# Reading token tiles spread by quarters and norming them in place, with a new order for the first attention step

## The chip, the cores and the metric

The kernel runs on one core of one Trainium2 chip. The metric is the device time of one execution in microseconds (us); smaller is better. Engines are named as in the profile: PE is TensorE (matmuls; PEld is its weight load), DVE is VectorE, ACT is ScalarE, POOL is GpSimd, SP is SyncE, which only issues DMAs. A "q" behind an engine's name is its sequencer, which issues DMAs and waits.

## The reference

Everything is float32; B = 2 sequences of S = 1024 tokens with H = 512 features, so 2048 tokens.

```
xn  = (x - mean(x)) / sqrt(var(x) + 1e-5)              # layernorm over the features
q, k, v = split(xn @ w_qkv.T + b_qkv)
s   = softmax(q @ k.T / sqrt(512)) @ v @ w_out.T + b_out
logits = xn @ router_w + router_b                      # 8 experts, the best two, softmax of the two
e_i = silu(xn @ expert_w[i] + expert_b[i])
c   = w_1 * e_1 + w_2 * e_2                            # weighted sum of the two chosen experts
y   = xn + c @ proj_w + proj_b
out = x + s * silu(norm_w * y / sqrt(mean(y*y) + 1e-6))
```

## The kernel before, in words

Tokens are worked in 16 tiles of 128. Each engine runs its instructions in the order in which the code writes them (`keep_order` ties each to the one before), so the order of the work is written out by hand, and what stands early in an engine's queue and waits holds all that stands behind it. DMAs are issued from SP, ACT and POOL in the same written order.

**Prologue (0 to 91 us).** SP loads the value and output weights (`wv_in`, `wo`), the query and key weights in spread form (`wZ`) and the token tiles `x`. TensorE transposes the value weights (`turn_wv`, L382) and multiplies them with the output weights (`product_vo`, L391: eight products, `hc` 0 to 3 for `n` 0 and then 1), so that values come out already projected; ACT copies each product from PSUM to `rwvo` (L402). `rwvo` also holds the router's weights and one more column. PSUM tiles of the pool `ps_mm` go round over four banks in written order.

The layernorm of a pair of tiles is `stats`, `shifts`, `rows` (L314 to L359). VectorE takes `bn_stats` and `bn_aggr` of each tile, ACT the root, VectorE reciprocal and shift; `rows` has ACT write the normed tile to `xn` with the features in another order (`in_turn`), and SP store it twice: to `xn_d`, from which the experts gather their tokens, and to the scratch `xn_s`, from which it comes back as `xz` with the tokens spread. For the first four tiles (`DIRECT`) there is no scratch: ACT writes a second normed copy `xw`, and TensorE transposes it. `turn_x` (L368) makes `xnT`, the tile with features on partitions: from `xz` by a 32x32 block transpose on VectorE (`turn`, L118), for the first four tiles from PSUM by a copy. `x` has 8 buffers, `xn` has 5 and `xz` has 6, so loads and norms wait for buffers.

`value_side` (L443) multiplies a tile by `rwvo` in two halves of 256 and 265 columns, PSUM tile `pv` with two buffers; `keep_values` (L458) copies the values to `vo` on ACT and adds the router's bias on VectorE to give the logits `lg`. `weighted` (L292) and `columns` (L303) make the bias terms: four VectorE steps, then matmuls with a column of ones (`pw`, `pu`). At tile 12 the expert weights `ew` (8 x 1 MB) start to load, then `eb`.

**Routing and queries (91 to 134 us).** VectorE ranks the tokens by expert while TensorE forms the query-key product (`product`, `queries`).

**Experts (134 to 255 us).** A pipeline over up to 39 slots of 128 rows (L803): POOL gathers rows of `xn_d`, SP puts them to scratch and takes them back spread, VectorE turns them to `gT`, TensorE multiplies by the chosen expert's weights (`ph`, L771), VectorE adds the bias, ACT applies silu and stores to `ho_d`.

**Attention (255 to 541 us).** Over pairs of tiles: scores by seven products instead of eight (`pair_scores`; `sum_left`, `sum_right` and `sum_values` make the operand sums), softmax, a turn of the probabilities through DRAM (`put`, `take_p`, `turn_p`), the product with the values (`attend`), and beside it the expert part: gathers from `ho_d` (`fetch`, POOL), weighting (`scale_c` on ACT, `combine` on VectorE), projection (`project`), `xr` read from `xn_d` with the bias added (`fetch_x`, `add_b`), root mean square, gate. The first pair is written out by hand in L1168 to L1193, ahead of the loop.

What decides the order around the change: SP's single queue for nearly all DMAs; ACT's queue, in which copies from PSUM, roots and norms stand in written order; and the written order of TensorE's products against VectorE's turns. The semaphore numbers that tell of a DMA's landing are handed out in turn to SP's and ACT's DMAs, eight of them, in written order.

Of the kernel before, what the change touches and what calls it, by code (L numbers as in the profile page):

```python
# [10 lines left out]
FP = mybir.dt.float32  # L11
# [9 lines left out]
P = 128  # L21
# [6 lines left out]
def kernel(  # L28
# [23 lines left out]
    G = 4  # L52
# [55 lines left out]

    QP = P // 4
# [22 lines left out]
    def turn_w(dst, z):  # L132
        for r in range(KC):
            dve.transpose(
                dst[:, :, ts(r, P)].rearrange("p j (i a) -> p i j a", a=QP),
                z[:, ts(r, 4), :].rearrange("p i (j b) -> p i j b", b=QP),
            )
# [31 lines left out]
    x = {}  # L169

    def load_x(t):
        x[t] = ln.tile([P, H], FP, tag="x", name=f"x{t}", bufs=8)
        sp.dma_start(x[t], x_d[:, t, :])
# [7 lines left out]
    def load_wv(c):  # L181
        sp.dma_start(wv_in[:, c, :], w_qkvT[ts(c, P), ts(2, H)])
# [12 lines left out]
    for t in range(2):  # L195
        load_x(t)
    load_wo(1)
    spread(sp, wZ[0], w_qkvT[:, ts(0, H)])
    for t in range(2, 4):
        load_x(t)  # L200
    sp.dma_start(rw[:, :, 0:E], router_w.rearrange("(c p) e -> p c e", p=P))
    for t in range(4, 8):
        load_x(t)
# [11 lines left out]
    make_identity(nc, ident)  # L215
    for q in range(4):
        for j in range(KC):
            gps.tensor_copy(bqk[ts(q, QP), :, j], bqkv[ts(j, QP), 0:2, q])
# [14 lines left out]
    mv = const.tile([P, NT, 2], FP, name="mv")  # L233
    std = const.tile([P, NT], FP, name="std")
    rstd = const.tile([P, NT], FP, name="rstd")
    shift = const.tile([P, NT], FP, name="shift")
# [55 lines left out]
    def weighted(w_, bias, name):  # L292
# [8 lines left out]
        return s_  # L301
# [10 lines left out]
    DIRECT = 4  # L312

    def stats(g):  # L314
        gs = ts(g, 2)
        for t in (2 * g, 2 * g + 1):
            st = ln.tile([P, 6], FP, tag="bnst", name=f"bnst{t}", bufs=4)
            dve.bn_stats(st, x[t])
            dve.bn_aggr(mv[:, t, :], st)
        act.activation(  # L320
            std[:, gs], mv[:, gs, 1:2].rearrange("p t o -> p (t o)"), AF.Sqrt, bias=ln_eps
        )

    def shifts(g):
        gs = ts(g, 2)
        dve.reciprocal(rstd[:, gs], std[:, gs])
        dve.scalar_tensor_tensor(
            shift[:, gs], mv[:, gs, 0:1].rearrange("p t o -> p (t o)"), -1.0, rstd[:, gs],
            ALU.mult, ALU.mult,
        )  # L330

    def normed(dst, src, t):
        act.activation(
            dst, src, AF.Identity, bias=shift[:, t : t + 1], scale=rstd[:, t : t + 1]
        )

    def direct(t):
        xw[t] = raw.tile([P, H], FP, tag="xw", name=f"xw{t}", bufs=DIRECT)
        normed(xw[t], x[t], t)

    def rows(g):

        two = (2 * g, 2 * g + 1)
        for t in two:
            xn_[t] = ln.tile([P, H], FP, tag="xn", name=f"xn{t}", bufs=5)
            normed(in_turn(xn_[t]), own(x[t]), t)
        if two[0] >= DIRECT:
            for t in two:
                xs[t] = dram.tile([4, P, P], FP, tag="xn_s", name=f"xn_s{t}", bufs=6)
                put(xs[t], xn_[t])  # L350
        for t in two:
            if t + 8 < NT:
                load_x(t + 8)
        for t in two:
            sp.dma_start(xn_d[ts(t, P), :], xn_[t])
        if two[0] >= DIRECT:
            for t in two:
                xz[t] = ln.tile([P, 4, P], FP, tag="xz", name=f"xz{t}", bufs=6)
                take(xz[t], xs.pop(t))  # L359

    def norm(g):
        stats(g)
        shifts(g)
        rows(g)

    xs, xz, xn_, xw = {}, {}, {}, {}

    def turn_x(t):  # L368
        dst = xnT[t // ST][:, :, ts(t % ST, P)]
        if t >= DIRECT:  # L370
            turn(dst, xz.pop(t))
            return
        ps = ps_mm.tile([P, 512], FP, tag="mm", name=f"xt{t}").rearrange(
            "p (j f) -> p j f", j=KC
        )
        for j in range(KC):
            pe.transpose(ps[:, j, :], xw[t][:, ts(j, P)], ident)
        dve.tensor_copy(dst, ps)
# [31 lines left out]
    stats(0)  # L410
# [3 lines left out]
    shifts(0)  # L414
    direct(0)
    product_vo(0, 3)
    direct(1)
    turn_w(wqkT[:, 0:KC], wZ[0])
    product_vo(1, 0)
# [3 lines left out]
    product_vo(1, 1)  # L423
    sq_ = weighted(wqkT[:, 0:KC], bqk[:, 1], "sq")
    product_vo(1, 2)
    turn_x(0)
    product_vo(1, 3)
    rows(0)
    turn_x(1)
    pbb = ps_mm.tile([P, 512], FP, tag="mm", name="pbb")  # L430
    pe.matmul(pbb[:, 0:KC], lhsT=ones, rhs=bb, start=True, stop=True)
    dve.tensor_reduce(rb[:, E:E1], pbb[:, 0:KC], AX.X, ALU.add)
    dve.tensor_copy(rw[:, :, E], columns(sq_, "pw"))
    stats(1)
    shifts(1)
    direct(2)
    direct(3)
    norm(2)


    pvs = {}

    def value_side(t):  # L443
        pv = ps_big.tile([P, 2, 512], FP, tag="big", name=f"pv{t}")
        pvs[t] = pv
        for n, cols in ((1, ds(HH + E1, HH)), (0, ds(0, HH + E1))):
            if n == 0 and t in (1, 2):
                turn_x(t + 1)
# [16 lines left out]
    for t in range(NT):  # L465
        if 3 < t < NT - 2:
            turn_x(t + 2)
# [852 lines left out]
```

## Time and profile before

| | |
|---|---|
| runs | 543.14, 543.22, 544.6 us; median 543.22 |
| the profiled execution's own time | 542.69 us |
| its span, first to last instruction | 541.0 us |
| granted TensorE clock, mean | 0.997 |
| DVE, ACT, POOL busy | 314.9, 156.9, 217.7 us |
| end of the value products | 91.14 us |
| first expert product | 134.45 us |
| last slot's filler product ends, attention's scores begin | 255.85 us |
| DMA over the span | 118.66 MB, 219 GB/s |

The profile's rows give start, duration, engine, source line, operation and the tiles out<-in. "x8" is a count of instructions, and one float32 matmul is two of them. A bracket holds the idle time of the engine before the row and what ended it. In the table of windows each engine's busy time and count stand first, then the granted TensorE clock (1.00 is full), the share of the 16 DMA engines and GB/s.

### The profile page before, as it was taken

To read this page: it belongs to the slowest core of one execution; us is meant where nothing else is said; L and a number is where in the kernel's file an instruction comes from. 1 tells how busy PE (TensorE), PEld (TensorE's weight loads), DVE (VectorE), ACT (ScalarE), POOL (GpSimd) and SP (SyncE) were. 2 spreads that over 40 slices of the span, in tenths; PEclk is the share of its full clock that TensorE was granted. 3 is DMA by queue.
4 is the path that set the end of the run, shared out by engine and by line. 5 is a ranking of instruction groups with operands and counts; after the bars stand their busy time and mean duration, and the time that the engine had idled before them with its cause. 6 is when DMAs were issued, how large, how long until landed. Compare 5 with 4: busy or idle time off the path is not lost.

```text
span 541.0 us, 5784 instructions
## 1 busy us (share of the span) xinstructions
PE 527.2 (97%) x1754; PEld 320.9 (59%) x1754; DVE 314.9 (58%) x529; ACT 156.9 (29%) x259; POOL 217.7 (40%) x231
## 2 busy tenths in 40 slices
PE   8979999999999999999999999999999999999996
PEld 6867887444444444444466666756746657484486
DVE  3645763841333333334689467376697685949595
ACT  2454312111211111111331622422425234152340
POOL 5000000023353874200276545346279755465551
PEclk9998999999999999999999999999999999999999
DMA  8879939939999999995566832723624628295502
GB/s 241 223 224 329 278 127 343 406 103 318 284 306 320 344 333 314 302 279 137 176 210 217 286 123 85 285 79 109 242 78 168 241 84 291 73 332 173 207 27 79
DMA packets 90928, 118.66 MB, mean 219 GB/s; under 512 B 6928, under 2 KB 55184, under 8 KB 90768
## 3 DMA queue, kind: packets, MB, share of 16 engines
q1 hardware_dynamic: 79344, 89.16, 51.4%
q0 software_dynamic: 5792, 18.88, 10.9%
q10 hardware_dynamic: 5760, 10.23, 5.0%
q8 instruction: 15, 0.25, 0.2%
q14 instruction: 17, 0.14, 0.1%
HBM read 73.69 MB, written 44.56 MB: 219 GB/s over the span
## 4 chain that ended last, share of the span: by engine, by line
PE 74%; DMA 10%; DVE 8%; issue 4%; ACT 1%; POOL 1%; SPq 1%; DVEq 0%; POOLq 0%; ACTq 0%
PE ph L771 20%; PE so L1104 17%; PE pp L1033 12%; PE po L970 10%; PE pq L512 5%; PE pv L450 4%; DMA wZ<-in_L_attn_w_qkv_dram 3%; PE pqk L543 3%; DMA xn_s<-xn 2%; PE pr L531 2%; DMA ho_d<-h 2%; DVE sc L1039 1%; DVE pT L120 1%; DMA xn_d<-xn 1%; DMA wo<-in_L_attn_w_out_dram 1%
## 5 line engine op out<-in xcount | busy, mean ns | idle before, releaser
L771 PE MATMUL ph<-ew,gT 128*128 x280 | 120.3, 592 | 0.0
L745 POOL DMA_INDIRECT xg<-xn_d,tok x39 | 37.2, 955 | 164.0 <-DVE npast L690 103.4
L771 PEld LDWEIGHTS ph<-ew,gT 128*128 128x128 f32 x280 | 53.2, 190 | 67.0 <-issue 67.0
L797 DVE TENSOR_TENSOR h<-ph,eb 128x512 f32<-128x512 f32 x39 | 26.9, 690 | 85.0 <-issue 53.1
L450 PE MATMUL pv<-rwvo,xnT 128*128 128x256 f32 (+1 forms) x256 | 60.3, 393 | 4.6 <-DVE lg L462 4.3
L450 PEld LDWEIGHTS pv<-rwvo,xnT 128*128 128x128 f32 x256 | 48.8, 194 | 15.0 <-DVE lg L462 6.3
L800 ACT ACTIVATE h<-h 128x512 f32<-128x512 f32 x39 | 24.6, 631 | 100.2 <-DVE h L797 97.4
L970 PE MATMUL po<-pw,ct 128*128 128x512 f32 x112 | 49.2, 592 | 0.0
L1001 ACT ACTIVATE pr<-sc,nm 128x1024 f32<-128x1024 f32 x16 | 18.3, 1146 | 89.5 <-DVE nm L998 78.4
L1111 DVE TENSOR_TENSOR o<-so,o 128x256 f32<-128x256 f32 x49 | 20.0, 421 | 39.2 <-PE so L1104 28.5
L1149 POOL TENSOR_TENSOR o<-o,base 128x512 f32<-128x512 f32 x14 | 20.6, 1491 | 47.6 <-DVE o L1114 47.6
L1033 PE MATMUL pp<-xnT,qT 128*128 128x512 f32 x84 | 39.5, 592 | 0.0
L1104 PE MATMUL so<-vo,pT 128*128 128x256 f32 x168 | 38.5, 379 | 0.0
L932 POOL DMA_INDIRECT hg<-ho_d,posi_m x32 | 32.4, 1014 | 13.2 <-issue 7.5
L970 PEld LDWEIGHTS po<-pw,ct 128*128 128x128 f32 x112 | 21.3, 190 | 25.5 <-issue 25.1
L1104 PEld LDWEIGHTS so<-vo,pT 128*128 128x128 f32 x168 | 31.9, 190 | 7.3 <-issue 2.6
L1039 DVE TENSOR_TENSOR sc<-pp,sc 128x512 f32<-128x512 f32 x49 | 31.6, 680 | 3.3 <-PE pp L1033 3.2
L120 DVE STREAM_TRANSPOSE gT<-sz 128x512 f32<-128x512 f32 x39 | 27.3, 701 | 7.1 <-DMA sz<-xs 7.1
L531 PE MATMUL pr<-xnT,wqk 128*128 128x256 f32 x128 | 29.2, 382 | 1.9 <-DVE sc L1039 1.9
L531 PEld LDWEIGHTS pr<-xnT,wqk 128*128 128x128 f32 x128 | 24.0, 190 | 8.1 <-DVE sc L1039 4.2
L120 DVE STREAM_TRANSPOSE pT<-pz 128x1024 f32<-128x1024 f32 x14 | 28.2, 2015 | 0.0
L512 PE MATMUL pq<-xnT,wqk 128*128 128x512 f32 x64 | 28.1, 594 | 0.0
(214 smaller groups left out, 773.0 us busy)
## 6 DMA issues: line engine op xcount, KB each, us to landing
xs<-xg SPq DMA_DIRECT2D x39, 256.0 KB, 4.7
sz<-xs SPq DMA_DIRECT2D x39, 256.0 KB, 4.7
ho_d<-h ACTq DMA_DIRECT2D x39, 256.0 KB, 4.9
ew<-in_L_ffn_expert_w_dram SPq DMA_DIRECT2D x8, 1024.0 KB, 13.4
ps<-pr SPq DMA_DIRECT2D x16, 512.0 KB, 2.9
pz<-ps SPq DMA_DIRECT2D x16, 512.0 KB, 4.9
x<-_attn_hidden_states_dram SPq DMA_DIRECT2D x16, 256.0 KB, 5.5
xn_d<-xn SPq DMA_DIRECT2D x16, 256.0 KB, 4.7
```

Source lines behind the costliest of these rows:

```text
L120: dve.transpose(dst.rearrange(f"p j {order} -> p i j a", a=QP), z.rearrange("p i (j b) -> p i j b", b=QP),)
L450: pe.matmul(pv[:, n, : HH + E1 * (1 - n)], lhsT=xnT[t // ST][:, c, ts(t % ST, P)], rhs=rwvo[:, c, cols], start=(c == 0), stop=(c == KC - 1),)
L512: pe.matmul(ps[:, half, :], lhsT=wqk[:, c, ts(oc, P)], rhs=xnT[0][:, c, ts(half, 512)], start=(c == 0), stop=(c == KC - 1),)
L531: pe.matmul(ps[:, :PW], lhsT=wqk[:, c, ts(oc, P)], rhs=xnT[1][:, c, ts(k, PW)], start=(c == 0), stop=(c == KC - 1),)
L745: gps.indirect_dma_start(out=xg[s], out_offset=None, in_=xn_d, in_offset=bass.IndirectOffsetOnAxis(ap=tok[:, s : s + 1], axis=0),)
L771: pe.matmul(ph, lhsT=g_[:, c, :], rhs=ew[:, ds(r, 1), c, :].rearrange("p e f -> p (e f)"), start=(c == 0), stop=(c == KC - 1),)
L797: dve.tensor_tensor(h, ph, eb[:, ds(r, 1), :].rearrange("p e f -> p (e f)"), ALU.add)
L932: gps.indirect_dma_start(out=g_, out_offset=None, in_=ho_d, in_offset=bass.IndirectOffsetOnAxis(ap=posi_m[:, n, t : t + 1], axis=0),)
L970: pe.matmul(po, lhsT=c_[:, c, :], rhs=pw[:, c, :], start=(c == 0), stop=(c == KC - 1))
L1033: pe.matmul(ps, lhsT=l_[:, c, :], rhs=r_[:, c, :], start=(c == 0), stop=(c == KH - 1))
L1039: dve.tensor_tensor(dst, ps, other, ALU.add)
L1104: pe.matmul(ps[:, :w_], lhsT=l_[:, c, :], rhs=r_[:, c, :], start=(c == 0), stop=(c == SK - 1),)
```

## The change

All 16 token tiles stay in one SBUF tile `x` of shape [128, 16, 4, 128]: partition 32q + a holds, of token 32i + a of a tile, the features 128q to 128q + 127. They are loaded in this form (four DMAs for each group of two or four tiles, in rows of 512 B, each into 32 partitions), so a tile's features are spread over four partitions. `parts` takes `bn_stats` of each piece of 128; `across` sums over the four partitions by a matmul with `eighth`; `means` and `variances` do so once for the means and once for the variances of a group of two or four tiles. ACT norms the tile in place in four pieces, SP stores it to `xn_d` from there, and `turn_x` turns it straight from `x`. The scratch `xn_s`, `xz`, `xn`, `xw` and TensorE's transposes of `xw` go.

Chunk j of `xnT` now holds the features 128q + 32j + b at partition 32q + b. Weights that meet it are loaded to match: `wv_in` (one DMA with other strides), the router's weights (four DMAs, on ACT's queue and not SP's), `ew` (four DMAs of 256 KB for each expert, each into 32 partitions, for one of 1 MB); `turn_w` writes its columns in another order. `wZ[1]` is loaded at the start and not at tile 4. The logits' bias is added once for all tiles and no longer tile by tile. The value products are written by halves, with the statistics' matmuls between them. In attention `xr`, `pb` and `y` are read in plain order, and the first pair's steps stand in another order.

```diff
+    x = ln.tile([P, NT, 4, P], FP, name="x")
+    def load_x(t, n):
+        for q in range(4):
+            sp.dma_start(
+                x[ts(q, QP), ds(t, n)].rearrange("p t i f -> p (t i) f"),
+                xr_d[ds(t * P, n * P), ts(q, P)].rearrange("(n a) f -> a n f", a=QP),
+            )
...
-    for t in range(2):
-        load_x(t)
+    load_x(0, 2)
     load_wo(1)
     spread(sp, wZ[0], w_qkvT[:, ts(0, H)])
-    for t in range(2, 4):
-        load_x(t)
-    sp.dma_start(rw[:, :, 0:E], router_w.rearrange("(c p) e -> p c e", p=P))
-    for t in range(4, 8):
-        load_x(t)
+    load_x(2, 2)
+    for q in range(4):
+        act.dma_start(
+            rw[ts(q, QP), :, 0:E], router_w[ts(q, P), :].rearrange("(j b) e -> b j e", b=QP)
+        )
+    for t in range(4, NT, 4):
+        load_x(t, 4)
+    spread(sp, wZ[1], w_qkvT[:, ts(1, H)])
...
+    def parts(t):
+        for i in range(4):
+            dve.bn_stats(st[:, t, i].rearrange("p h k -> p (h k)"), x[:, t, i, :])
+    def means(t, n):
+        dve.tensor_reduce(mean[:, g_], across(at_[:, :, :, 1], f"pmean{t}"), AX.X, ALU.add)
+        dve.tensor_tensor(dev[:, g_], at_[:, :, :, 1], ..., ALU.subtract)
+        dve.tensor_tensor(dev[:, g_], dev[:, g_], dev[:, g_], ALU.mult)
+        dve.scalar_tensor_tensor(dev[:, g_], at_[:, :, :, 2], 8.0 / H, dev[:, g_], ALU.mult, ALU.add)
+    def variances(t, n):
+        dve.tensor_reduce(var[:, g_], across(dev[:, g_], f"pvar{t}"), AX.X, ALU.add)
+        act.activation(std[:, g_], var[:, g_], AF.Sqrt, bias=ln_eps)
+        dve.reciprocal(rstd[:, g_], std[:, g_])
+        dve.scalar_tensor_tensor(shift[:, g_], mean[:, g_], -1.0, rstd[:, g_], ALU.mult, ALU.mult)
+    def norm(t):
+        for i in range(4):
+            act.activation(x[:, t, i, :], x[:, t, i, :], AF.Identity, bias=..., scale=...)
+    def store(t):
+        for q in range(4):
+            sp.dma_start(xn_d[...], x[ts(q, QP), ds(t, 2)].rearrange("p t i f -> p (t i) f"))
...
-    stats(0)
+    parts(0)
+    parts(1)
     product_vo(0, 1)
     turn_wv(3)
     product_vo(0, 2)
-    shifts(0)
-    direct(0)
+    means(0, 2)
     product_vo(0, 3)
-    direct(1)
+    variances(0, 2)
+    norm(0)
+    turn_x(0)
+    product_vo(1, 0)
+    norm(1)
+    turn_x(1)
+    product_vo(1, 1)
+    store(0)
     turn_w(wqkT[:, 0:KC], wZ[0])
...
+    value_half(0, 1)
+    means(2, 2)
+    next(sum_q)
+    value_half(1, 1)
+    variances(2, 2)
+    norm(2)
...
+    sq_ = next(sum_q)
+    dve.tensor_reduce(rb[:, E:E1], pbb[:, 0:KC], AX.X, ALU.add)
+    dve.tensor_copy(rw[:, :, E], columns(sq_, "pw"))
+    value_half(0, 0)
...
+    for t in range(2, NT):
+        if 2 < t < NT - 1:
+            turn_x(t + 1)
+        value_half(t, 1)
+        keep_values(t - 1)
+        if t in (2, 5, 9):
+            first = {2: 4, 5: 8, 9: 12}[t]
+            means(first, 4)
+        value_half(t, 0)
+        if t in (2, 5, 9):
+            variances(first, 4)
+        if t + 2 < NT:
+            norm(t + 2)
+            if t % 2:
+                store(t + 1)
+        if 3 <= t < 7:
+            parts(2 * t + 2)
+            parts(2 * t + 3)
...
             for e in range(E):
-                sp.dma_start(ew[:, e], expert_w[e].rearrange("(c p) f -> p c f", p=P))
+                for q in range(4):
+                    sp.dma_start(
+                        ew[ts(q, QP), e],
+                        expert_w[e, ts(q, P), :].rearrange("(j b) f -> b j f", b=QP),
+                    )
...
+    sum_left(1)
+    both_of(fetch, 0)
     keys, vals = sum_right(0), sum_values(0)
     for _ in range(2):
         next(keys)
-    sum_left(1)
-    both_of(fetch, 0)
-    sp.dma_start(pb, proj_b.partition_broadcast(P))
-    both_of(fetch_x, 0)
-    both_of(add_b, 0)
-    sp.dma_start(nw, norm_w.partition_broadcast(P))
     scores(0)
     next(keys)
     for _ in range(3):
         next(vals)
     take_p(0)
+    sp.dma_start(pb, proj_b.partition_broadcast(P))
+    both_of(fetch_x, 0)
+    both_of(add_b, 0)
+    sp.dma_start(nw, norm_w.partition_broadcast(P))
     scores(1)
     close(ps_guard)
     ps_guard, ps_s = pool("ps_s", bufs=4, space=PSUM)
     tw[0] = next(keys)
+    both_of(inverse, 0)
+    tv[0] = next(vals)
+    queries_of(0, lambda name: ps_mm.tile([P, 512], FP, tag="mm", name=name))
     both_of(scale_c, 0)
-    both_of(inverse, 0)
     both_of(combine, 0)
-    tv[0] = next(vals)
     take_p(1)
     both_of(take_c, 0)
     both_of(fetch, 1)
-    queries_of(0, lambda name: ps_mm.tile([P, 512], FP, tag="mm", name=name))
```

## The prediction

> **What bounds the kernel now.** I read the page first (parts 1, 2 and 4), then TensorE's timeline from end to end, then the four engines and SyncE's queue over the first 95 us, the queue's own waits, the windows, and last the stretch 240 to 300 us.
>
> ```profile
> PE 527.2 (97%) x1754; PEld 320.9 (59%) x1754; DVE 314.9 (58%) x529; ACT 156.9 (29%) x259; POOL 217.7 (40%) x231
> ```
>
> TensorE works 527.2 of 541.0 us. Its 13.8 idle us are few, so they can be listed: 1.2 before the first matmul, 4.2 after the last, and waits. The largest is where the value products meet the layernorm's round trip through DRAM:
>
> ```profile
> 34.21 1.95 PE L450 MATMUL pv<-rwvo,xnT 128*128 128x265 f32 x8
> 39.55 5.47 PE L450 MATMUL pv<-rwvo,xnT 128*128 128x256 f32 x16 [3.40 <-DVE lg L462]
> 45.26 7.45 PE L450 MATMUL pv<-rwvo,xnT 128*128 128x256 f32 x32 [0.23 <-DVE xnT L120]
> ```
>
> The bracket is the idle time before the row. The releaser named is VectorE, but behind it stands ScalarE, held until 38.02 for a buffer that a store to xn_d had to leave. The row itself is dear too: 16 matmuls take 5.47 us; at the usual step of 0.2155 us (6.87 us for 32) they take 3.45. The windows say why:
>
> ```profile
> 35.00:40.00 5.00, 1.60 (x8) 1.06 (x7) 0.77 (x3) 1.28 (x2) 0.00 (x0) 0.99 0.97 310
> 40.00:45.00 5.00, 5.00 (x16) 3.70 (x14) 2.43 (x9) 2.28 (x4) 0.00 (x0) 0.66 1.07 376
> ```
>
> The third number from the end is the granted clock: 0.66 after the pause. So that wait cost 3.4 + 2.0 us. From the end of tile 2's products (36.0) to the end of them all (91.14) pass 55.1 us; 13 tiles x 16 x 0.2155 = 44.8, 0.8 for the nine extra columns and 1.7 for `pu` and `pvb` make 47.3. **7.8 us are to be had there**, and 0.55 before `pw`.
>
> **Part 1: loads and stores by quarters.** The spread load exists before: `wZ` (512 B rows into 32 partitions). `pw` has its form with 2 KB rows.
>
> ```profile
> 12.00:16.00 4.00, 4.00 (x20) 3.54 (x19) 0.77 (x3) 3.59 (x7) 0.00 (x0) 1.00 1.24 194
> 65.00:66.00 1.00, 1.00 (x6) 0.89 (x5) 1.00 (x3) 1.00 (x2) 0.00 (x0) 1.00 1.05 400
> 161.00:165.00 4.00, 4.00 (x11) 1.79 (x10) 1.31 (x2) 0.63 (x1) 0.86 (x1) 1.00 1.08 229
> ```
>
> The last number is GB/s: `wZ` alone (12 to 16) 194, rows of 2 KB in 128 partitions 400, `pw` 229. The Trainium skill ("DMA: Bandwidth & Descriptors", Specifications) puts line rate at 512 B and more; by it 256 KB of x would still take 0.65 us and nothing would move. By the row of the same shape it is 1.4 us; I take the row. So x0 and x1 take 2.8 us, not 1.36, and the last quarter of `wZ[0]` lands at 17.67 + 1.5 = 19.2 (before: 17.67). Tiles 2, 3 land by 22, 4 to 7 by 27.7, all by 39: ahead of their use below. Against that, 24 DMAs of the round trip (6.3 MB) go.
>
> **Part 2: the router's four loads move to ScalarE's queue.** This is the dear step. SyncE's own waits show a rule of this program:
>
> ```profile
> SPq L173 <- DMA wZ<-in_L_attn_w_qkv_dram: 2.8, 3, 1.2
> ```
>
> (Total us, times, longest.) Loads of x share no data with `wZ`. Yet those issued at 13.75, 14.59 and 16.13 each came just after a `wZ` quarter landed (13.39, 14.57, 16.11). Eight completion semaphores go round over SyncE's and ScalarE's DMAs in written order (`wo`'s second half, the ninth, waits for `bqkv`, the first, which ScalarE issued), so each DMA waits for the eighth before it. In the changed order `bqkv` is 1, `wv` and `wo(0)` 2 to 6, x0/x1 7 to 10, `wo(1)` 11, `wZ[0]` 12 to 15, x2/x3 16 to 19, the router 20 to 23. The 23rd waits for the 15th: the last `wZ[0]` quarter, 19.2. ScalarE's copies of `pvo` are queued behind it. The first then comes at 19.2 + 0.35 (issue) + 1.28 (table load, which stood right after ScalarE's DMA before) = 20.85. `ps_mm` has four banks; counting them off, `product_vo(0, 2)` needs the first `pvo`'s bank. It began at 11.53 and now begins at 21.2: **+9.7 us**. Bounds: 0 if ScalarE is not held, 10.5 if `wZ` comes at 20. The pause drops the clock: +1.9 by the 2.0 of the row above; the skill ("TensorE: Matmul & The Clock Gate", Part 1) has half rate for about 3.4 us, 1.7.
>
> **Part 3: statistics and norm.** From `product_vo(0, 2)` to the end of tile 2's products TensorE needed 36.0 - 11.53 = 24.5 us. Out: four times four transposes, 1.75 (0.44 a tile), and the 0.55 wait. In: five sums over partitions at 0.15 (the `pk` pair steps 0.14), 0.75. That is 22.9. VectorE: four `bn_stats` of 128 columns have no row; between 0.18 (the aggregate's) and 0.27 (0.668 less 384 columns at 1.04 ns), I take 0.2, nearer independent issue; a group's `means` is four small dependent operations at 0.2 = 0.8, `variances` 0.75 with the root on ScalarE. `turn_x` drops from 1.10 to 0.70, gT's row of the same write order. Norm becomes four ScalarE operations of 128 columns: 0.22 to 0.33 each by the 128x256 copy (0.37), 1.0 a tile, 0.8 before.
>
> Laid on the clock: last `product_vo` ends at 33.8. VectorE does the two first transposes till 32.05, `turn_w` 2.5, eight `bn_stats` 1.6, so tile 2's mean matmul waits from 35.5 to 36.35 (0.85), and with it everything queued behind it on TensorE, the value products of tile 1 first. Then two steps of `sq` 1.25, means 0.8, a step 0.77, variances 1.0, the last step 0.8: `pw` waits from 38.75 to 41.0 (2.25), and the half behind it for the copy into `rw` (0.3). Tiles 4 to 7: 0.6. Sum 4.0; 0 to 6 with `bn_stats` at its bounds. Tile 2 ends at 21.2 + 1.9 + 22.9 + 4.0 = 50.0, **+14.0**. After it the 7.8 us of waits go (xnT needs no round trip; x stays in place, so no buffer is waited for), and six sums at 0.15 come: **-6.9**. End of the value products: **+7.1**, at 98.2.
>
> The `lg` add at the end (0.3, plus a 0.2 copy, for 0.17) is covered: VectorE had the ranks ready at 97.02 and TensorE asked at 98.0. With that cover gone it costs 0.3. GpSimd's seven small operations for `eighth` end long before 24. The 32 stores of 128 KB are written on SyncE behind all loads of x and `wZ[1]` (landed by about 45); nothing on the path reads them before the gathers.
>
> **Part 4: the expert weights and the last store.** 32 DMAs of 256 KB replace eight of 1 MB. At `pw`'s rate 256 KB take 1.2 us, in all 38.4 (21.7 before). They start as before 10.4 us ahead of the end of the value products (T), land at T - 10.4 + 2.6 + 38.4 = T + 30.6. `store(14)` is written after them on SyncE and adds 4 x 0.6 = 2.4. The gathers read all of xn_d, so the first cannot start before T + 33.1; it started at T + 24.0 (115.15). Its chain had slack:
>
> ```profile
> 126.16 0.71 DVE L120 STREAM_TRANSPOSE gT<-sz 128x512 f32<-128x512 f32 x1 [5.01 <-DMA sz<-xs]
> ```
>
> gT is ready at 126.87, the first expert matmul starts at 134.45: 7.6. So 9.1 - 7.6 = 1.5, plus `eb` (2 MB, right behind) in the gather's way: 0 to 2.5, I take 2.0. A wait of 3.5 is as long as the one that dropped the clock, +1.9: **+5.4** (0 if the loads run at 400 GB/s, 9 at 1.35 us a quarter). The later slots come every 2 to 3.3 us, under an expert's 3.43.
>
> **Part 5: the first attention step.**
>
> ```profile
> 284.12 1.98 PE L1033 MATMUL pp<-tw,qT 128*128 128x512 f32 x4 [0.60 <-ACT sc L1041]
> 293.98 3.72 PE L531 MATMUL pr<-xnT,wqk 128*128 128x256 f32 x16 [0.91 <-DVE sc L1039]
> ```
>
> The first wait comes from ScalarE standing at `scale_c` until the gathers land (281.42) with four `qT` copies queued behind; with the copies ahead it goes (-0.6). VectorE then runs about 0.5 earlier; the other wait falls to the 0.45 of later pairs. `pb`, the two `xr` and `nw` move on SyncE behind `take_p(0)` (273.85) and land near 278, before `add_b` (279.27 on GpSimd, behind the same four gathers). **-1.0**; 0 to -1.5.
>
> **The sum.** +7.1 + 5.4 - 1.0 = +11.5 on the profiled execution (542.69, span 541.0): 554.2. The median of the runs is 543.22, 0.5 more: 554.5.
>
> **Rivals.** (a) ScalarE is not held: the router's waits are met early. 11.6 us fall away and, with the expert wait below the clock's drop (2.7), it ends at 540.5, **faster**. It decides once the hold is under about 2.7 us. For it: no row shows ScalarE itself held in the prologue. Against: its stores of `ho_d` stand behind the same kind of wait on the same eight semaphores. (b) Held, but the expert weights come in time, several quarters moving at once: 549. Against: `pw`'s four quarters, also issued together, ran at 229 GB/s. (c) Everything as said but VectorE has no new waits: 550.5.
>
> **Chances.** My case 0.5; (b) and (c) 0.27; worse than 560 (`eb` and gathers collide) 0.1; (a) 0.13. Under (a) most is faster, some within 0.3% (1.6 us, about what a measurement of this kernel tells from no change). Faster 0.10, same 0.04, slower 0.86. Range 544 to 562; my own case 551 to 558.
>
> **What would show it.** Right: an idle TensorE from about 11.5 to 21 released by ScalarE, clock near 0.6 after it; value products ending near 98 without long waits after 50; `ew` landing over some 38 us; a wait before the first expert product. Wrong: `pvo` copied at 9 us as before, or VectorE's small operations dearer than 0.2, or gathers not waiting for `store(14)`.

## The result, and the profile after

| | before | after |
|---|---|---|
| median of the runs (both made on the same chip), us | 543.67 | 577.84 (571.89 to 578.45) |
| the profiled execution's own time, span | 542.69, 541.0 | 577.64, 575.9 |
| end of the value products (T) | 91.14 | 105.40 |
| first expert product | 134.45 | 171.50 |
| start of attention's scores | 255.85 | 292.90 |
| from there to the end | 285.15 | 283.0 |
| DMA over the span, MB | 118.66 | 112.38 |

The changed kernel is slower by 6.0% (ratio 1.0602, 95% interval 1.053 to 1.0674). That is 34.9 us of span: +14.3 up to the end of the value products, +22.8 from there to the first expert product, nothing over the experts, -2.1 in attention. I had said +11.5 (+7.1, +5.4 and -1.0), so the direction and the three stretches were right; the sizes were not, and in the first two stretches the time was lost to something other than what I had named.

Part 1 of the page of after, beside the line of before that opens the prediction: TensorE is busy 10 us longer (most of it slow clock), and its idle time grows from 13.8 to 38.3 us. The second line is the clock in 40 slices of 14.4 us: it drops in two places, slices 4 and 10 to 11.

```profile
PE 537.6 (93%) x1758; PEld 327.1 (57%) x1758; DVE 310.7 (54%) x565; ACT 167.5 (29%) x316; POOL 215.7 (37%) x238
...
PEclk9997999995699999999999999999999999999999
```

TensorE's waits in after, in total us, times, longest. Two of them make most of the idle time, and neither is one that I had priced: the wait for `lsel` in the routing, and the one for the value weights.

```profile
PE ptok L706 <- DVE lsel L698: 18.6, 4, 17.4
PE wvt L399 <- DMA wv_in<-in_L_attn_w_qkv_dram: 7.0, 3, 4.4
PE pmean L344 <- DVE st L338: 2.5, 2, 1.6
PE pw L331 <- DVE sq L322: 1.6, 1, 1.6
...
PE pv L457 <- DVE xnT L120: 1.0, 1, 1.0
```

The last row is the only wait of the value products for `xnT` (before: 3.40 at that place, 0.23 and more), and it is not the round trip's (part 3 below): that part of the change did what it says.

**The prologue.** TensorE's timeline, first two rows of before, then after:

```profile
3.78 1.09 PE L387 MATMUL wvt<-ident,wv_in 128*128 128x128 f32 x4
...
11.53 8.80 PE L395 MATMUL pvo<-wo,wvT 128*128 128x256 f32 x40
```

```profile
8.29 1.09 PE L399 MATMUL wvt<-ident,wv_in 128*128 128x128 f32 x4 [4.37 <-DMA wv_in<-in_L_attn_w_qkv_dram]
...
21.07 0.63 PE L399 MATMUL wvt<-ident,wv_in 128*128 128x128 f32 x4 [2.14 <-DMA wv_in<-in_L_attn_w_qkv_dram]
21.54 1.89 PE L407 MATMUL pvo<-wo,wvT 128*128 128x256 f32 x8
25.00 0.36 PE L344 MATMUL pmean<-st,eighth 128*128 128x16 f32 x2 [1.56 <-DVE st L338]
...
28.24 8.12 PE L407 MATMUL pvo<-wo,wvT 128*128 128x256 f32 x32
...
43.15 1.24 PE L331 MATMUL pw<-ones,sq 128*128 128x1 f32 x8 [1.57 <-DVE sq L322]
44.64 8.54 PE L457 MATMUL pv<-rwvo,xnT 128*128 128x265 f32 x24 [0.26 <-DVE rwvo L481]
```

The row at 21.54 is `product_vo(0, 2)`, which I had put at 21.2. It is there for another reason: the first transpose of the value weights waits for its data until 8.29, the fourth until 21.07. ScalarE, which I said would be held until 19.2, is not. Its timeline (ACTq rows are DMA issues) shows the four router loads issued between 1.23 and 3.70, the table load right behind, and then a wait for TensorE:

```profile
1.23 2.47 ACTq L209 DMA_DIRECT2D rwvo<-in_L_ffn_router_w_dram  x4
3.72 1.28 ACT L414 ACT_TABLE_LOAD   x1 [3.72 <-issue]
16.61 0.37 ACT L414 COPY rwvo<-pvo 128x256 f32<-128x256 f32 x1 [11.61 <-PE pvo L407]
```

**The middle.** TensorE in after, then VectorE in before and in after, then SyncE's queue in after:

```profile
119.80 7.03 PE L549 MATMUL pq<-xnT,wqk 128*128 128x512 f32 x16
144.20 0.72 PE L706 MATMUL ptok<-tsel,lsel 128*128 128x80 bf16 x8 [17.37 <-DVE lsel L698]
...
148.12 9.58 PE L549 MATMUL pq<-xnT,wqk 128*128 128x512 f32 x16
...
171.50 8.75 PE L808 MATMUL ph<-ew,gT 128*128 x20
```

```profile
102.18 1.49 DVE L640 TENSOR_TENSOR hsel<-iota,hi 128x1280 bf16<-128x1280 f32 x1
```

```profile
138.59 1.49 DVE L677 TENSOR_TENSOR hsel<-iota,hi 128x1280 bf16<-128x1280 f32 x1 [22.09 <-DMA xn_d<-x]
```

```profile
95.05 32.89 SPq L533 DMA_DIRECT2D ew<-in_L_ffn_expert_w_dram  x32
128.96 3.95 SPq L384 DMA_DIRECT2D xn_d<-x  x4
138.51 0.36 SPq L542 DMA_DIRECT2D eb<-in_L_ffn_expert_b_dram  x1
```

Read from the bottom up: the last store of `x`, `store(14)`, is written behind the 32 expert loads and is issued only at 128.96. `hsel`, a tile of the ranking, lies in memory that `x` has to leave first, so VectorE stands from 116.5 to 138.59. `lsel` and with it `ptok` come behind, and TensorE waits 18.6 us. The `pq` products behind it begin at half clock (0.50 from 140 to 150 us) and take 9.58 instead of 7.11. In before the same `hsel` ran at 102.18 without a wait: its stores had been issued long ahead of `ew`.

### The profile page after: what moved, and what is told of

Read it like the earlier page. It is cut to its first block, busy times and chain, and to the rows that moved or that the text cites. A ratio compares the mean times of both kernels' runs of the same rounds, so it can differ in the third digit from the quotient of the medians.

```text
span 575.9 us, 5914 instructions
## 1 busy us (share of the span) xinstructions
PE 537.6 (93%) x1758; PEld 327.1 (57%) x1758; DVE 310.7 (54%) x565; ACT 167.5 (29%) x316; POOL 215.7 (37%) x238
## 2 busy tenths in 40 slices
DMA packets 95857, 112.38 MB, mean 195 GB/s; under 512 B 7248, under 2 KB 65744, under 8 KB 95696
## 4 chain that ended last, share of the span: by engine, by line
PE 76%; DMA 13%; DVE 7%; issue 2%; ACT 0%; SPq 0%; DVEq 0%
PE ph L808 19%; PE so L1141 16%; PE pp L1070 13%; PE po L1007 10%; PE pv L457 7%; DMA ew<-in_L_ffn_expert_w_dram 6%; PE pq L549 4%; PE pr L568 4%; DMA wv_in<-in_L_attn_w_qkv_dram 3%; PE sc L1051 2%; DMA wZ<-in_L_attn_w_qkv_dram 1%; DMA xn_d<-x 1%; DMA x<-_attn_hidden_states_dram 1%; DVE lsel L698 1%; DVE sc L1076 1%
## 5 line engine op out<-in xcount | busy, mean ns | idle before, releaser
L457 PE MATMUL pv<-rwvo,xnT 128*128 128x256 f32 (+1 forms) x256 | 62.3, 400 | 1.3 <-DVE xnT L120 1.0
L549 PE MATMUL pq<-xnT,wqk 128*128 128x512 f32 x64 | 30.6, 636 | 0.0
L568 PE MATMUL pr<-xnT,wqk 128*128 128x256 f32 x128 | 28.8, 381 | 0.9 <-DVE sc L1076 0.9
```

The source lines that it names most:

```text
L457: pe.matmul(pvs[t][:, n, : HH + E1 * (1 - n)], lhsT=xnT[t // ST][:, c, ts(t % ST, P)], rhs=rwvo[:, c, cols], start=(c == 0), stop=(c == KC ...
L549: pe.matmul(ps[:, half, :], lhsT=wqk[:, c, ts(oc, P)], rhs=xnT[0][:, c, ts(half, 512)], start=(c == 0), stop=(c == KC - 1),)
L568: pe.matmul(ps[:, :PW], lhsT=wqk[:, c, ts(oc, P)], rhs=xnT[1][:, c, ts(k, PW)], start=(c == 0), stop=(c == KC - 1),)
```

## The experiments

Times are medians; each ratio is against the kernel before on the same chip. The medians of before on these chips lie between 542.30 and 543.67, so a difference between runs of different sets is good to about 1.4 us. The traces are of one execution each.

**1. Value weights by 128 rows.**

```diff
-            w_qkvT.rearrange("(q j b) o -> j q b o", q=4, b=QP)[c][:, :, ts(2, H)],
+            w_qkvT[ts(c, P), ts(2, H)],
```

> The changed kernel, but the value weights are loaded as before (128 rows in a line for each DMA, and not four groups of 32 rows); the features then stand in another order than those of xnT, so the values are not the reference's. Theory A: the changed kernel starts late because a wv_in load whose source pattern has an outermost count of four moves some 70 to 100 GB/s and not 400. Then the first transpose comes at about 4 us (8.3 in the changed kernel), the fifth product (n 0, hc 2) at 12 to 14 us (21.5), the value products end at 95 to 97 (105.4), and the time is 567 to 570 us. Rival B: the start is late because the four router loads on ScalarE and the spread loads of x fill the eight completion semaphores and the engines; then the value products end no earlier than 103 and the time stays at 575 to 578.

562.45 us, 1.0377 (1.0302 to 1.0453): 15.4 less than after. `product_vo(0, 2)` starts at 10.55, and the value products end at 90.90 where after has 105.40. The router's loads are still on ScalarE and the statistics are as changed. Time and end of the value products lie below what theory A said (567 to 570, 95 to 97). Part of that is chance: the prologue of experiments 4, 6, 10 and 13 is the same up to the expert loads, and there the value products end at 95.40, 93.48, 94.75 and 92.62. So the pattern of four loads makes the prologue's loss, and the long wait in the middle is untouched:

```profile
10.55 1.89 PE L404 MATMUL pvo<-wo,wvT 128*128 128x256 f32 x8
...
90.90 7.03 PE L577 MATMUL pqk<-qT 128*128 128x512 f32 x16
...
128.30 0.71 PE L703 MATMUL ptok<-tsel,lsel 128*128 128x80 bf16 x8 [15.97 <-DVE lsel L695]
```

**2. The store ahead of the expert loads**: the loop of loads is written at tile 13, behind `store(14)`.

```diff
+        if t == 13:
             for e in range(E):
                 for q in range(4):
                     sp.dma_start(ew[ts(q, QP), e], ...)
```

> The changed kernel, but the expert weights are written at tile 13, after the last store of x to xn_d, and not at tile 12 ahead of it. Theory C: VectorE's 22 us before hsel are the release of x's memory, whose last reader is that store behind 32 loads; then the wait goes, TensorE's 17.4 us before ptok and the slow clock after it go too, and the time is 555 to 558 us. Rival D: hsel waits for the expert weights' traffic itself (or for the end of eb), whatever the order; then the wait stays over 15 us and the time over 572.

556.94, 1.0276 (1.0212 to 1.034): 20.9 less than after. `ptok` has no wait at all; in its place 2.73 us come before the first expert product (149.48).

**3. The expert weights as eight loads of 1 MB**, the store still behind them.

```diff
-                for q in range(4):
-                    sp.dma_start(ew[ts(q, QP), e], ...)
+                sp.dma_start(ew[:, e], expert_w[e].rearrange("(c p) f -> p c f", p=P))
```

> The changed kernel, but each expert's weights are loaded as before by one DMA of 1 MB into 128 partitions (their features then stand in another order than the tokens', so the experts' products are not the reference's); the last store still stands behind them. Theory C with the rate: the weights pass in 22 us instead of 40, the store lands some 18 us earlier against the value products' end, hsel waits 3 to 5 us instead of 22 and ptok under 3: 557 to 560 us. Rival E: the number of DMAs (32 against 8) and not the 32 partitions sets the 40 us, which this run cannot tell from C; but if the wait has nothing to do with the weights the time stays over 572.

558.32, 1.0301 (1.024 to 1.0362). `ptok` waits 4 x 0.67 us instead of 18.6 in all, `hsel` 5.4 instead of 22.1. Either edit thus removes all or most of the same stall: it needs the slow loads and the store behind them. What makes these loads slow, their number or the 32 partitions (rival E), is taken up with experiment 13.

**4. Edits 1 and 2 together.**

> The edits of the first two kernels of this set together (value weights loaded as before, so the values are not the reference's; expert weights written after the last store). If the two delays are separate and one after the other, they add: 546 to 549 us. If the late start only hides in the later wait (one covers the other), it is the smaller of the two alone, 555 or more.

549.47, 1.0134 (1.0088 to 1.018): 28.4 less than after, not 15.4 + 20.9, and just above the 546 to 549 expected. (The profiled execution, 552.4, was the slowest of five.) TensorE's timeline has a new wait, and SyncE's queue has its cause: behind `ew` and `eb` the puts of gathered rows (`xs`) take until 140 to come back (`sz`).

```profile
143.76 46.42 PE L806 MATMUL ph<-ew,gT 128*128 x102 [4.89 <-DVE gT L120]
```

```profile
122.92 0.35 SPq L540 DMA_DIRECT2D eb<-in_L_ffn_expert_b_dram  x1
128.94 5.36 SPq L112 DMA_DIRECT2D xs<-xg  x3
140.07 0.34 SPq L116 DMA_DIRECT2D sz<-xs  x1
```

The packets of `eb` run until 138.8, in the way of the puts. Part 4 of my prediction had a wait at this place (3.5), but mainly by another way: there the gathers wait for the last store. Here they start at 119.41, 24.0 behind the end of the value products as in before, and the puts behind them are late. The wait shows only when the other stalls are gone.

**5. Only the new order of the first attention step**, on the kernel before (the last hunk of the diff).

> The kernel before with only the new order of the first attention step. My prediction's step put it at -1.0 us (0 to -1.5); the trace of the changed kernel, from the start of attention's scores to the end, is 2.1 shorter than before. If the order alone makes that, 543.2 - 2.1 = 541.1, and TensorE shows neither the 0.60 before the fourth group of pair products nor the 0.91 before the keys' products. Rival: the 2.1 come from the plain order of xr, pb and y (GpSimd's add and VectorE's add without the strided views); then this kernel gains only my 1.0 or less: 542.2 to 543.2.

540.97, 0.9964 (0.9946 to 0.9981): 0.4% below before, beyond the interval, and as expected (541.1). From the start of the scores to the end 282.96 us pass (before 285.15, after 283.0), so the order makes all of attention's gain and the plain layout of `xr` and `y` none. Both waits are gone (the rows at 284.12 and 293.98 in before):

```profile
282.75 1.88 PE L1033 MATMUL pp<-tw,qT 128*128 128x512 f32 x4
...
287.90 7.07 PE L531 MATMUL pr<-xnT,wqk 128*128 128x256 f32 x32
```

**6. Edits 1, 2 and 3.**

> The changed kernel with the value weights by 128 rows and the expert weights written behind the last store, and now also loaded as eight DMAs of 1 MB; rows of both weights stand in another order than the tokens' features, so the output is not the reference's. It differs from the run with the first two edits (549.47, wait of 4.89 before the first expert product, clock 0.64 to 0.68 after it) only in the form of the expert loads. If that wait is the quarters' rate (39 us for 8 MB, the gathers' puts and eb behind them on SyncE), it goes, and with it 4.9 + about 2.5 of slow clock: 542 to 543, first expert product about 7 us earlier at 138.5 or less after value products that end where they did. Rival: the wait is eb and the gathers' own traffic whatever the form of the expert loads; then 547 to 549.

543.81, 1.0012 (0.9997 to 1.0027): no difference from before (542 to 543 was expected). The wait of 4.89 is gone, and from the end of the value products (93.48) to the first expert product pass 43.31 us, exactly as in before. So the three edits account for the whole loss. What is left is a prologue 2.3 us longer than before's and attention 2.15 shorter. The 2.3 hold on average too: the five profiles with this prologue end their value products at 93.4, and before and experiments 5 and 8, which have before's, at 91.1.

**7. The value weights' pattern alone**, on the kernel before.

> The kernel before with only the source pattern of the four value weight loads changed to the one of the changed kernel (four groups of 32 rows); the value products then see rows in another order than the tokens' features, so the output is not the reference's. My theory: with four groups outermost each DMA keeps about four packets in flight and 1 MB takes some 11 us; the first transposes start near 8.3 and product_vo(0, 2) near 21 where it was 11.53, less what was waiting for tokens anyway (0.55 before pw and the slack of the xw chain), and the pause drops the clock: +9 to +12, 552 to 555. Rival (my prediction's step): the load costs nothing and the prologue's delay came from ScalarE's router loads and VectorE: 543.2.

555.42, 1.023 (1.0185 to 1.0274). The counterpart of the first experiment: with nothing else changed, and with the router's load on SyncE as in before, `product_vo(0, 2)` moves from 11.53 to 21.92 and the value products end at 103.85.

```profile
8.07 1.09 PE L390 MATMUL wvt<-ident,wv_in 128*128 128x128 f32 x4 [4.14 <-DMA wv_in<-in_L_attn_w_qkv_dram]
...
21.92 1.89 PE L398 MATMUL pvo<-wo,wvT 128*128 128x256 f32 x8
```

**8. The expert weights by quarters alone**, on the kernel before.

> The kernel before with only the expert weights loaded by quarters (32 DMAs of 256 KB into 32 partitions each for eight of 1 MB into 128); their rows then stand in another order than the tokens' features, so the output is not the reference's. No store stands behind them here. My theory: 39 us for 8 MB instead of 22, eb and the gathers' puts behind them on SyncE, a wait of about 5 before the first expert product and slow clock after it: +5 to +7, 548.5 to 550.5. Rival: it costs only with a store queued behind; then 543 to 544.

545.62, 1.0043 (1.0023 to 1.0064): both theories missed. The loads run at 217 to 220 GB/s from 81.31, the first `sz` is issued at 131.68 where before has 122.8, and `gT` is ready 8.4 us later. The slack of 7.6 us that I had read in before takes up nearly all of it; 0.23 us are left:

```profile
135.36 55.05 PE L775 MATMUL ph<-ew,gT 128*128 x127 [0.23 <-issue]
```

The profiled execution (544.09) shows 0.5 us before the end of the value products, 0.4 from there to the first expert product and 0.4 over the experts; the rest of the median's 2.4 I did not locate. In experiment 4 the same loads start at 88.35, because there they stand behind a store that waits for the last norm; counted from the end of the value products that is 3.3 us later. The quarters cost little by themselves; the quarters with a later start cost 4.89 and the clock behind it.

**9. One `xn` buffer more** (and one `xz` less), with the new attention order, on the kernel before.

> The kernel before with the new order of the first attention step, six xn buffers for five and five xz for six (the same memory). My reading of before: ScalarE stood 3.05 us at tile 7's norm for the buffer that tile 4's store had to leave (landing 37.91), and TensorE paid 3.40 + 2.0 for it. With one buffer more that norm waits for tile 3's store (29.20, long landed). The turn of tile 4 then waits for its own round trip (39.28), so some 1.5 to 2 of the 5.4 stay: -2.1 - 3.5 = about 537.5; 541.1 if the stall only moves to the round trip (rival).

541.12, 0.9963 (0.9948 to 0.9979), the same as experiment 5: the rival was right. The 3.05 us that ScalarE stood are gone, but the waits pass to the round trip itself, and the value products end at 91.74:

```profile
44.46 3.75 PE L450 MATMUL pv<-rwvo,xnT 128*128 128x256 f32 x16 [1.90 <-DVE xnT L120]
49.27 3.78 PE L450 MATMUL pv<-rwvo,xnT 128*128 128x256 f32 x16 [1.06 <-DVE lg L462]
```

**10. Expert quarters on two queues**, on experiment 4.

```diff
-                    sp.dma_start(
+                    (gps if q % 2 else sp).dma_start(
```

> The run with value weights by rows and the store ahead (549.47), with every second quarter of the expert weights issued by GpSimd, which has no work between 88 and 113 us; value weight rows as there, so the output is not the reference's. Theory A: about 210 GB/s is what one group of 32 partitions takes, and two queues write two groups at once: 8 MB in about 22 us, the wait before the first expert product goes, 543 to 545 as with the 1 MB loads (543.81). Theory B: the limit is of this form of transfer whatever the queue, 39 us again: 549 to 550.

543.52, 1.0016 (0.9998 to 1.0033): the wait is gone, as theory A has it, but not for its reason. The traffic rises from about 211 to 224-311 GB/s in windows of 4 us (three of them are shown with experiment 13), not to 400; and GpSimd's queue, which no store holds, starts at 84.67, where SyncE's starts at 87.82 here and at 88.35 in experiment 4. The last expert load is issued at 114.00, not 120.95. What each of the two causes contributes was not separated.

**11. The changed kernel mended**: value weights in eight loads with 32 rows outermost, four of them on ScalarE's queue; the store ahead; expert quarters on two queues; the rest as changed.

```diff
+    def load_wv(h):
+        for q in range(4):
+            (act if q % 2 else sp).dma_start(wv_in[ts(q, QP), ts(h, 2), :],
+                w_qkvT[ts(q, P), ts(2, H)].rearrange("(j b) o -> b j o", b=QP)[:, ts(h, 2)])
```

> The changed kernel mended with the right rows: value weights in eight DMAs of 128 KB, one for each quarter of features and half of the chunks (32 rows outermost), quarters 1 and 3 on ScalarE's queue; the expert weights behind the last store, every second quarter on GpSimd's queue; all else as changed. Theory A (two queues write two groups of partitions at once): first transpose of the value weights near 5, product_vo(0, 2) near 12, value products ending near 95, no wait before the first expert product: 544 to 546. Theory B (the form is the limit): first transpose near 6, product_vo(0, 2) near 14, and the expert wait stays: 550 to 553. ScalarE issues nine DMAs ahead of its first copy here; if that holds it, as my prediction had it of the router loads, the first pvo copy comes later than 10 in either case.

545.01, 1.0034 (1.0011 to 1.0057). First transpose at 6.64 and `product_vo(0, 2)` at 14.22 as theory B had them; no expert wait, value products ending at 94.71 and the time as A. Here ScalarE was held by its own loads: nine of them, the last issued at 9.02, the first `pvo` copied at 11.82. That cost nothing, since the product to be copied ended at 11.78.

**12. VectorE's bias chain out of the prologue**, on experiment 6: `turn_w` moves to tile 6; `sq` and `pw` are left out.

> The run with both weights by rows and the store ahead (543.81, value products ending at 93.48) with VectorE's bias chain taken out of the prologue: the turn of the query weights is moved to tile 6, and the four steps of sq and pw are left out (their column is zero); so the output is not the reference's. If VectorE's work between 20 and 33 makes the waits of 1.86, 1.57 and 0.26 and the slow clock after them (0.79 in 30 to 35), as part 3 of my prediction had it, they go, and pw's 0.9 too: value products ending at 87 to 88.5, 538 to 539.5. Rival: the waits pass to ScalarE's norms or to the loads of tokens, 541 to 543.

538.52, 0.9926 (0.9898 to 0.9954); value products end at 87.84. Expected was 87 to 88.5, so VectorE's chain between 20 and 33 us is what holds the new prologue (0.9 us of the gain is `pw` itself, which this run leaves out on TensorE). The rival is right in part: `pmean` still waits 1.28, behind a load of tokens for which VectorE stands 1.70, the later one 1.51 (1.04 in experiment 6), and two waits for ScalarE's `lg`, 0.76 and 1.24, are new. But these short waits no longer slow the clock:

```profile
20.00:30.00 10.00, 8.72 (x43) 7.34 (x42) 3.84 (x19) 3.64 (x11) 0.00 (x0) 1.00 1.22 215
30.00:40.00 10.00, 8.49 (x41) 6.98 (x39) 6.14 (x26) 4.94 (x16) 0.00 (x0) 1.00 1.23 202
```

**13 and 14. The two queues write different halves of the partitions**, on experiments 10 and 11: `q > 1` in place of `q % 2`.

> As the run with expert quarters on two queues (543.52), but GpSimd issues quarters 2 and 3 (partitions 64 to 127) and SyncE quarters 0 and 1, where before it was 1 and 3 against 0 and 2; value weights by rows, so the output is not the reference's. There the traffic rose only from about 211 to 238-269 GB/s, not to 400. The Trainium skill (SBUF - State Buffer, Door 1: The DMA port swizzle) has partitions 0 to 63 on eight of 16 ports and 64 to 127 on the other eight. If that is the limit, two queues now write different halves: 370 to 400 GB/s in the first 10 us of both, the last expert load issued at about 102 to 106 and not 114; the time stays at 543 to 544.5, since no wait was left before the first expert product. If the form's limit is elsewhere, 230 to 270 GB/s again.

> As the mended kernel with two queues (545.01), with quarters 2 and 3 of the value weights on ScalarE's queue and those of the expert weights on GpSimd's, so that at each time both halves of the partitions are written. Computes the reference. By the port rule the value weights' first half lands about 1 us earlier: first transpose near 5.5 where it was 6.64, value products ending near 93.5; 543.5 to 544.5. If the partitions written at once do not matter: 545.

543.15, 1.002 (1.0004 to 1.0036), and 544.02, 1.0031 (1.0004 to 1.0059). Windows of experiment 10, then of 13, while both queues load:

```profile
90.00:94.00 4.00, 4.00 (x20) 3.44 (x19) 0.00 (x0) 0.65 (x2) 1.96 (x4) 1.00 1.08 311
94.00:98.00 4.00, 4.00 (x13) 2.13 (x12) 2.02 (x7) 0.65 (x2) 1.10 (x2) 1.00 1.04 228
98.00:102.00 4.00, 4.00 (x13) 1.91 (x12) 2.67 (x11) 2.16 (x4) 0.55 (x1) 1.00 1.05 264
```

```profile
90.00:94.00 4.00, 4.00 (x17) 2.90 (x16) 0.39 (x2) 0.65 (x2) 2.10 (x4) 1.00 1.07 284
94.00:98.00 4.00, 4.00 (x11) 1.81 (x10) 3.51 (x13) 0.32 (x1) 1.10 (x2) 1.00 1.04 288
98.00:102.00 4.00, 4.00 (x15) 2.13 (x14) 2.52 (x11) 2.24 (x4) 0.00 (x0) 1.00 1.04 292
```

That is 288 GB/s on average instead of 268 (experiments 14 and 11: 287 and 270), against about 211 from one queue; experiment 10 swings, and in one window is above 13. The last expert load is issued at 111.66, not at the 102 to 106 expected. The mended kernel's first transpose comes at 5.73 instead of 6.64. (In experiment 11 the trace puts the end of that wait down to GpSimd's `bqk` copies; in 14 these run as long and TensorE starts earlier, so it does not need them.) The halves matter a little, but 370 to 400 was not reached, so the partitions written at once are only a part of the limit. The rest stays open.

The trace's packet records settle rival E of experiment 3. From 92 to 118 us of experiment 4 some 17 packets are under way all the time, and from 84 to 94 us of before, with loads of 1 MB, some 16. But a packet of 2 KB takes 164 ns on average in the one and 87 in the other. So the 32 loads keep the queue full, and their number is not what slows them. With two queues a packet takes 137 ns (experiment 10, 90 to 102 us), with different halves 123.

## Why the prediction was wrong, point by point

Two steps failed. The four `wv_in` loads were put at nothing, and they delay the prologue by 10 us. And the last store was thought to hold up the gathers, where it first holds up `hsel`, and through it TensorE for 18.6 us.

**The loads of x and `wZ` by quarters (part 1): right size, incomplete.** The estimate of 190 to 230 GB/s into 32 partitions held: 204 to 220 in the windows of after from 30 to 50 us. What failed is the step that I did not take: `wv_in` ("one DMA with other strides") was costed at nothing. In the windows of after the kernel moves 72 and 96 GB/s while little but those loads and the router's small rows is open; before has 305 from 4 to 8. Before, then after:

```profile
4.00:8.00 4.00, 3.35 (x18) 2.70 (x18) 1.38 (x2) 0.00 (x0) 3.28 (x28) 1.00 0.90 305
```

```profile
7.00:8.00 1.00, 0.00 (x0) 0.00 (x0) 0.00 (x0) 0.00 (x0) 0.94 (x13) 1.00 0.35 72
8.00:9.00 1.00, 0.71 (x4) 0.74 (x5) 0.00 (x0) 0.00 (x0) 0.92 (x4) 1.00 0.27 96
45.00:50.00 5.00, 5.00 (x12) 3.83 (x12) 1.72 (x9) 1.43 (x5) 0.00 (x0) 0.50 1.16 204
```

The DMA share in the two rows from 7 to 9 is 0.35 and 0.27, that is 4 to 6 of 16 engines. In the packet records SyncE's queue has 3.9 packets under way from 8.0 to 9.5, all of 2 KB and of 84 ns (median); before has 16.8 from 7.0 to 8.5, and its packets of 2 KB take 84 ns too. So each packet is as fast as before, and there are four at a time. The Trainium skill ("DMA: Bandwidth & Descriptors", Rules for kernel authors) says that an outermost dimension of c < 16 confines a DMA to at most c engines; here c is 4, and row and rule agree. It was in the skill, and I had not weighed it: rows stayed 2 KB, so I took the load as unchanged. An estimate by the rule: at before's 305 GB/s 1 MB takes 3.4 us, on a quarter of the engines 13.8, so 10.3 more; `product_vo(0, 2)` came 10.0 later. That the two are so near is luck in part: the fourth load landed only near 21, some 19 us after the first was started and not 13.8. Other loads run beside the four; what they take was not separated.

**The router's loads on ScalarE (part 2): wrong, though its number was met.** I had completion semaphores handed out in written order over both engines and so ScalarE held until `wZ[0]` landed. The four loads were issued by 3.70 us. The order is not the written one, as I also had it in the description of the kernel before, where a single load on ScalarE at the start does not tell the orders apart. The hold exists, but on the other queue. In after SyncE waits 4.8 us for the first `wv_in` load to land before it issues the fourth, the sixth DMA in written order:

```profile
SPq L188 <- DMA wv_in<-in_L_attn_w_qkv_dram: 4.8, 1, 4.8
```

The trace's semaphore numbers show why: the router's four loads had taken four of the eight by then, and the fourth `wv_in` load has the first one's again. This does not set the start: in experiment 7, without these loads on ScalarE, the fourth is issued at 3.70 and not at 8.17, and `product_vo(0, 2)` starts as late. The +9.7 was measured as +10.0 from `wv_in`. A match of a number is no proof of its reason: had only TensorE's row at 21.54 been read, the step would have passed. Experiment 1 removes the delay with the router's loads where they are.

**VectorE and the clock (part 3): the waits right in sum, the clock too small.** From the start of `product_vo(0, 2)` to the end of tile 2's products after took 33.7 us (21.54 to 55.21); I had 28.8. The new waits are 1.56, 0.23, 0.89, 1.57 and 0.26, together 4.5; I had 4.0. The sum agrees in part by luck: the first two, 1.79, I did not have (VectorE's first `bn_stats` stands 5.27 us for the loads of tokens and starts at 23.20), `pw`'s 1.57 was 2.25 with me, and the 0.6 of tiles 4 to 7 did not come. The `bn_stats` of 128 columns follow each other at 0.2 us, as taken; the norm of a tile takes 1.65 and not 1.0, and no wait of TensorE shows it. The slow clock is the term that was mis-sized, 1.9: beside the same rows of experiment 12, which ran at full clock, the products took 0.6 (2.57 for 1.97), 1.0 (8.12 for 7.15) and 3.0 (8.54 for 5.55) more, and `pw` 0.2 more than in before, 4.8 in all. Of the 4.9 that I was short, 2.9 are thus clock and 0.5 waits; the other 1.5 I did not trace. One pause was priced, and there were several in a row; the clock was 0.68 in 25 to 30, and 0.50 all through 45 to 50 (the row above), after waits of 0.89 and 1.57 that alone are short. From the end of tile 2 on -6.9 was said and -4.9 measured (50.2 us for 55.1): a wait of 1.0 for `xnT` came new at tile 11, whose turn on VectorE (85.15) stands behind the four steps of `sk` (from 82.39); the other 1.0 I did not trace.

So the 7.8 us that I had found in the round trip are real, but most of them go to VectorE: with every load mended (experiment 6) the value products end 2.3 later than before; with the bias chain away they end 3.3 earlier.

**Expert weights and the last store (part 4): the place failed.** I saw that `store(14)` stands behind 38 us of loads, and I charged it to the gathers, where 7.6 us of slack lay. I did not ask who else waits for that store: a store reads `x`, and `x` gives its memory to `hsel`, which VectorE starts 13 us ahead of the gathers (102.18 and 115.15 in before). What I had charged to the gathers, 3.5 and 1.9 of slow clock, is near what experiment 4 shows at the first expert product, 4.89 and some 2.5, but that is luck in part: there the gathers are on time and the puts are late behind `ew` and `eb`. In after this cost was hidden behind the larger stall.

**Attention (part 5): right mechanism, half the size.** -1.0 was said, -2.1 measured (-2.2 in experiment 5). I left 0.45 of the second wait standing; it went whole (0.91), and later pairs' waits went from 0.45 and 0.49 to 0.45 and 0.44. Together with 0.60 that names 1.6; the rest is spread over products that ran slightly slower behind those waits (1.98 for 1.88 in the row at 284.12) and I did not trace it further.

**The rivals.** (a), ScalarE not held, was right in its premise and wrong in its outcome, since the prologue's delay had another cause. (b) and (c) did not occur.

## What to carry to other kernels

When a load's source is re-ordered, look at its outermost count and not only at the length of its rows: the four loads with a 4 outermost cost 12 to 15 us here (experiments 7 and 1), the same bytes with 32 outermost and two queues some 3 (`product_vo(0, 2)` at 13.60 for 10.55). When a store is put behind a long run of loads in a queue, list everything that waits for it, and count the tile that takes over its memory among them: here that came 13 us ahead of the reader that I had checked. And a shared engine that "has room" must have it at the moment: taking 24 DMAs away moved the bound of the prologue to VectorE.

## What the runs showed of the hardware that was not expected

- Loads into 32 partitions ran at some 204 to 221 GB/s from one queue whether their rows were 512 B or 2 KB; two queues reached 268, and 288 when they wrote partitions below and above 64 at the same time, against 386 to 398 for 128 partitions from one queue (experiment 6, 90 to 106 us).
- Two loads can be slow in two ways: few packets at a time, each at its usual 84 ns (3.9, `wv_in` in after), or as many as ever, each slower (17 at 164 ns, `ew` by quarters).
- Short waits can slow the clock as a long one does: behind waits of 0.89, 1.57 and 0.26 us in after it was 0.50 over 5 us, behind one of 3.40 in before 0.66. But waits of 1.28 and 1.51 ten us apart (experiment 12), and of 1.90 and 1.06 five us apart (experiment 9), left it at 1.00. A rule does not come out of these runs.
